# Moving pieces of side work in a two-layer graph network kernel: the last outputs' loads, eight bias additions, two loads of x

## The chip, the cores and the metric

One core of one Trainium2 chip. The metric is the device time of one execution in microseconds (us); the kernel before took a median of 1796.12 us in 3 runs (1794.81 to 1798.48).

## The reference, cut to what matters

```python
# x: (16, 1024, 128), adj: (1024, 1024), all float32
h = relu(layernorm(x))
x = x + (adj @ (h @ weight) + bias)               # layer 0
h = relu(layernorm(x))                            # layer 1
for _ in range(5):
    m  = adj @ h                                  # per batch: (1024,1024) @ (1024,128)
    av = concat([m, m])
    u3 = h @ u3_w.T + u3_b
    z  = sigmoid(av @ w3_w.T + w3_b + u3)
    r  = sigmoid(av @ w4_w.T + w4_b + u3)
    hv = tanh(av @ w5_w.T + w5_b + (r * h) @ u5_w.T + u5_b)
    h  = (1 - z) * h + z * hv
return x + h
```

## The kernel before, in words

The 16 batches go in four quads of four. Two quads are in work at a time and take turns, so that one quad's squares can travel to DRAM and back while the other computes. `step` (L789 on) is one round of one quad; it is written here as (quad, round). The order is (0,0), (1,0), (0,1), (1,1) and so on to (1,4), then (2,0), (3,0) and on to (3,4), which is the last. Within (0,1) and (1,3) an extra aggregation of layer 0 for quads 2 and 3 stands after the gates (`BLOCKS`).

A step has two stages. **The aggregation** (`aggregate`, L436 on) multiplies by adj with two levels of Strassen's scheme: 7 large products, each of 7 small ones, 49 in all (`SMALL`). A small product is 4 matrix multiplications (two 128x256 ones, each in two passes in the trace). Their left sides ("big", "little") are sums that VectorE makes just ahead of use; their right sides are precomputed. Nine of the right sides stay in SBUF ("resident"). The other 40 are streamed from DRAM as 20 pairs of 512 KB through a ring that holds six pairs: `stream()` (L294) issues the next load after every second streamed product. When an aggregation begins, its first six pairs are there, and it issues the loads of the other fourteen itself and, unless it is the last, of the next one's first six. ScalarE takes each result out of PSUM (L519), and VectorE adds it up into mT (L238). Large product 5 of 7 has three such additions of 1024 columns in a row, before which and after which "little" sums of the next products stand. **The gates** (`gates`, L711 on) are 20 multiplications of 512 columns (two passes each) with the weights for each half of the quad, A and then B, with Sigmoid and Tanh on ScalarE and products and sums on VectorE; at their end the new h is transposed in 32x32 squares by VectorE (L581, "sq") and stored to DRAM ("fn").

Side work is put among all this by hand. `put(k, piece)` books a piece, and `place(k)` emits it: `place(1)` to `place(49)` follow the small products of the aggregation, `place("Ar0")`, `"Az3"`, `"Br0"` and the like follow the units of the gates (r for the reset gate, z for the update gate, number of the unit 0 to 3). All that is emitted stays in program order on its engine, and every DMA is issued by SyncE (SP), in order.

The side work that the change touches:

- `put_statistics` (L678 on): layer norm for a coming quad's batches (8 to 15 in its form "a"), the statistics in the gates of one step, the ReLU in the aggregation of the next step. After it, the bias of layer 0 is added to the batch's x (`bias`, L647: one VectorE addition of 1024 columns, "xt<-xt,gb"), at places 26 and 36 of that same aggregation. This happens in (1,0), (0,1), (0,3) and (1,3).
- `LOADS` (L83): loads of later batches' x.
- In the step (3,4), "final": the outputs of quad 2 (`output`, L627). Each has three pieces. load: the last h comes back from DRAM in four gathering DMAs of 128 KB ("ho<-fn"), and x in one of 512 KB ("xt<-x1d"); rest: x is added ("xt<-xt,ho", two additions on VectorE); store. The load of the first stands in the gates of (2,4) ("Bz1"). The flip pool, from which "ho" and "sq" are taken, has three buffers.
- `squares` of the fourth batch of a quad is booked for place 3 of the next aggregation, and the stores of the third and fourth batch's squares for places 4 and 9 (in `turn`, L838).

Of the kernel before, what the change touches and what calls it, by code (L numbers as in the profile page):

```python
# [47 lines left out]
def _small_products():  # L48
# [33 lines left out]
}  # L82
LOADS = {  # L83
    (0, 0): ((8, 25), (9, 34), (10, 43), (11, "Ar0")),
    (0, 2): ((12, 26), (13, 40)),
    (1, 2): ((14, 26), (15, 40)),
}
TRANSPOSED = {(1, 0): 1, (1, 4): 2, (3, 0): 3}
OUTPUTS = {(3, 0): 0, (2, 1): 1, (3, 1): 2, (2, 2): 3, (3, 2): 4, (2, 3): 5, (3, 3): 6, (2, 4): 7}
# [4 lines left out]
def tile_two_gnn_layers(  # L94
# [30 lines left out]
    def dma(out, in_):  # L125
        pin(nc.sync.dma_start(out=out, in_=in_))
# [4 lines left out]
    def x_tile(b):  # L131
        return pre.tile([P, NC, D], F32, tag="xt", name=f"xt_{b}")

    def load_x(b, xt=None, parts=((0, NC),)):
        xt = xt if xt is not None else x_tile(b)
        for cs in parts:
            cs = slice(*cs)
            dma(xt[:, cs], by_slots(x[b])[:, cs])
        return xt
# [97 lines left out]
    def add(o, a, b):  # L237
        pin(nc.vector.tensor_add(o, a, b))  # L238
# [190 lines left out]
    def early_pieces(n):  # L429
        bigs, smalls = left_pieces(n)  # L430
        return bigs[0] + smalls[0] + bigs[1] + bigs[3]

    def period(i):
        return 2 + 7 * i
# [132 lines left out]
    def flip_tile(nm):  # L567
        return flip.tile([P, NSQ, NC, SQ], F32, tag="sq", name=nm)
# [34 lines left out]
    def transposing(b, hT):  # L603

        box = {}

        def load():
            box["sq"] = flip_tile(f"sqt_{b}")
            dma(box["sq"].rearrange("p k j e -> p (k j e)"), parked[b][0])

        def turn():
            for g in range(NH):
                pin(nc.vector.transpose(transposed_half(hT, g), squares_of_half(box["sq"], g)))

        return load, turn
# [4 lines left out]
    def put(k, *pieces):  # L620
        fixed.setdefault(k, []).extend(pieces)
# [25 lines left out]
    def bias(b):  # L647
        both = gb.unsqueeze(1).to_broadcast([P, NC, D])
        add(xts[b], xts[b], both)
# [28 lines left out]
    def put_statistics(kind, first):  # L678

        rest = []  # L680
        for n, b in enumerate((first, first + 1)):
            box = {}

            def begin(b=b, box=box):
                box["n"] = Norm(xts[b], None, f"{kind}{b}")
                box["n"].statistics(range(CH))

            def relu(k, b=b, box=box):
                def run():
                    if k == 0:  # L690
                        box["n"].dst = flip_tile(f"h{kind}_{b}")
                    box["n"].relu(range(2 * k, 2 * k + 2))

                return run

            def done(b=b, box=box):
                (keep if kind == "a" else layer_1_input)(b, box["n"].dst)

            key = "AB"[n]
            put(f"{key}r3", begin)  # L700
            put(f"{key}z1", lambda box=box: box["n"].statistics(range(CH, NC)))
            put(f"{key}z3", lambda box=box: box["n"].scales(EVERY))
            rest.append((10, lambda box=box: box["n"].shift(EVERY)))
            rest += [(11 + 13 * n + 3 * k, relu(k)) for k in range(CH)]
            rest.append((22 + 14 * n, done))
            if kind == "a":
                rest.append((26 + 10 * n, lambda b=b: bias(b)))
        return rest


# [73 lines left out]
    def loads_of_next(source, places):  # L784

        for k, at in enumerate(places):
            put(at, lambda k=k: natural_from(source[k], nat[:, k]))

    def step(i, loads_at=(period(4), period(5), "Ar0", "Ar2"), early_places=GATE_PLACES):  # L789
        st = state[i]  # L790
        quad, n = st["quad"], st["step"]
        nm = f"{quad}_{n}"
        hT = [hT_all[:, i, k] for k in range(Q)]
        last = n == STEPS - 1
        final = last and quad == quads - 1
        other = state[1 - i]
        me = (quad, n)
        for k, piece in relus.pop("next", ()):
            put(k, piece)
        for b, k in LOADS.get(me, ()):  # L800
            put(k, lambda b=b: xts.update({b: load_x(b)}))
        if me in TRANSPOSED:
            q = TRANSPOSED[me]
            for k in range(Q):
                load, turn_it = transposing(q * Q + k, hT_all[:, q % 2, k])
                put(8 + 10 * k, load)
                put(17 + 10 * k, turn_it)
        if me in OUTPUTS:
            for k, piece in zip((16, 34, 38), outputs[OUTPUTS[me]]):
                put(k, piece)  # L810
        block = BLOCKS.get(me)

        source = h0_of(block) if block else other["blocks"]
        if final:
            st["x1"] = []

            def load_x1(k):
                x1 = x_tile(f"1_{quad * Q + k}")
                dma(x1, x1s[quad * Q + k])
                st["x1"].append(x1)  # L820

            for k, places in enumerate(((None, 10, 13), (2, 18, 21), (15, 28, 31), (24, 40, 43))):
                for piece, at in zip(outputs[(quad - 1) * Q + k], places):
                    if at is not None:
                        put(at, piece)
            for k, at in enumerate((17, 34, "Ar0", "Ar3")):
                put(at, lambda k=k: load_x1(k))
        if source is not None:
            loads_of_next(source, loads_at)
        aggregate(nm, place)  # L830
        if me in NORMS:
            relus["next"] = put_statistics(*NORMS[me])
        if source is not None:
            for k, piece in zip(early_places, early_pieces(made[0])):
                put(k, piece)
        stored, ready = {}, {}

        def turn(first):  # L838
            def run(k):
                k += first  # L840
                stored[k] = Later(lambda n: ready[k][n])

                def squares():
                    store, ready[k] = squares_to_dram(hT[k], f"{nm}_{k}")
                    if k >= Q - 2:
                        put({Q - 2: 4, Q - 1: 9}[k], store)
                    else:
                        store()

                if k == Q - 1:  # L850
                    put(3, squares)
                else:
                    squares()

            return run

        if last:
            outputs.update({quad * Q + k: output(quad * Q + k, Later(lambda n, k=k: ready[k][n])) for k in range(Q)})
            if quad == quads - 2:
                put("Bz1", outputs[quad * Q][0])  # L860
        for a, key in enumerate("AB"):
            pair = slice(2 * a, 2 * a + 2)
            if final and a == 1:
                for k, (load, rest) in enumerate(final_outputs(quad, st, stored)):
                    put(f"Br{2 * k}", load)
                    put(f"Bz{2 * k + 1}", rest)
            gates(
                [mT[:, 2 * a + k] for k in range(2)],
                hT[pair],
                f"{nm}{key}",  # L870
                key,
                turn(2 * a),
                finish=finish(quad, hT[pair], st) if final and a == 1 else None,
            )
        if final:
            st["quad"], st["blocks"] = None, None
            return
        st["step"] += 1
        st["blocks"] = [stored[k] for k in range(Q)]
        if last:  # L880
            begin(i, quad + 2)
        if block:
            loads_of_next(other["blocks"], (period(3) + 4, period(4) + 4, period(5) + 2, period(6)))
            pieces = early_pieces(made[0] + 1)
            for k, piece in zip(BLOCK_PLACES, pieces):
                put(k, piece)
            aggregate(f"a{block}", place)
            for k in range(Q):
                for g in range(NH):
                    po(block * Q + k, g)  # L890
                    if 2 * k + g in (1, 2, 6, 7):
                        pieces[{1: 6, 2: 7, 6: 8, 7: 9}[2 * k + g]]()
# [4 lines left out]
    def begin(i, quad):  # L897

        if quad >= quads:
            state[i] = {"quad": None, "blocks": None}  # L900
            return
        state[i] = {"quad": quad, "step": 0, "blocks": parked_of(quad)}
# [13 lines left out]
    def h0_of(quad):  # L916
        return Later(lambda k: h0_blocks[quad * Q + k])
# [151 lines left out]
    for k in range(Q):  # L1069
        b = Q + k  # L1070
# [56 lines left out]
```

## Time and profile before

| | |
|---|---|
| median of 3 runs | 1796.12 us |
| profiled execution | 1800.02 us, of it 1798.2 us span |
| TensorE busy | 1776.1 us (99%) |
| VectorE, ScalarE busy | 1364.2 us (76%), 901.3 us (50%) |
| mean DMA rate | 220 GB/s |
| gates, both halves | 34.34 us |
| aggregation without a wait of TensorE | 42.36 us |

The gates' first multiplications (line L720, "pr") stand in the chain of work that ended last. From one such start to the next is one step's length:

| step | from | to | length | over 76.70 |
|---|---|---|---|---|
| most | 1208.49 | 1285.18 | 76.69 | 0 |
| (1,0) | 176.71 | 257.32 | 80.61 | 3.91 |
| (0,1) | 257.32 | 334.95 | 77.63 | 0.93 |
| (0,2) | 461.17 | 539.98 | 78.81 | 2.11 |
| (1,2) | 539.98 | 616.91 | 76.93 | 0.23 |
| (0,3) | 616.91 | 694.53 | 77.62 | 0.92 |
| (1,3) | 694.53 | 772.16 | 77.63 | 0.93 |
| (1,4) | 898.52 | 976.40 | 77.88 | 1.18 |
| (3,0) | 1053.10 | 1131.79 | 78.69 | 1.99 |
| (3,4) | 1668.70 | 1752.21 | 83.51 | 6.81 |

The names in a row of the trace leave out buffer and batch numbers, so "ring<-rd" is any load of the ring and "pr_4A" any quad's round 4, half A. "x4" is the number of instructions merged in a row. In square brackets stands the idle time of the engine before the row and what ended it.

### The profile page before, as it was taken

Reading aid. Unit: us, or ns where it says so; the run is one execution under the profiler, and the core shown is the slowest. Engines: PE = TensorE matmul, PEld = TensorE weight load, DVE = VectorE, ACT = ScalarE, POOL = GpSimd, SP = SyncE. Lnnn points to the kernel's source line nnn. Section 1 sums busy time; section 2 is a strip of 40 time slices with the busy share of each in tenths; the row PEclk is TensorE's granted clock in tenths of the full one; section 3 lists DMA queues with packets and bytes.
Section 4 is the critical chain, followed back from the end, with each engine's and each line's share of the span. In section 5 each row is a group of like instructions: output and inputs, shape, how many; then the busy total and the mean of one; then the engine's idle time right before and its main releaser. Section 6 shows DMA issues by size and latency. Waiting matters only on the chain.

```text
span 1798.2 us, 21453 instructions
## 1 busy us (share of the span) xinstructions
PE 1776.1 (99%) x6466; PEld 1208.7 (67%) x6466; DVE 1364.2 (76%) x2793; ACT 901.3 (50%) x1969; POOL 57.3 (3%) x41
## 2 busy tenths in 40 slices
PE   9999999999999999999999999999999999999998
PEld 3558576678585766758857667585675857668574
DVE  5758879676878697877687968778686776877776
ACT  5226555544555655554455554545455454454534
POOL 2101000000000000000000000000000000000000
PEclk9999999999999999999999999999999999999999
DMA  6399684678485956649839477494865849577592
GB/s 219 132 340 307 220 294 155 209 221 250 150 276 171 313 170 207 228 134 287 254 125 340 160 238 253 157 324 134 243 214 173 276 140 286 169 217 244 159 333 94
DMA packets 168866, 396.36 MB, mean 220 GB/s; under 512 B 18480, under 2 KB 86960, under 8 KB 168752
## 3 DMA queue, kind: packets, MB, share of 16 engines
q1 hardware_dynamic: 168752, 395.00, 68.0%
q8 instruction: 52, 0.85, 0.2%
q14 instruction: 62, 0.51, 0.1%
HBM read 314.18 MB, written 80.74 MB: 220 GB/s over the span
## 4 chain that ended last, share of the span: by engine, by line
PE 91%; DVE 4%; DMA 3%; issue 1%; ACT 1%; POOL 0%; SPq 0%; DVEq 0%; POOLq 0%; ACTq 0%
PE a L500 25%; PE c L500 12%; PE b L500 6%; PE pq_a L543 4%; PE a_a L500 3%; PE pr_0A L720 2%; PE pr_3B L720 2%; PE pr_2A L720 2%; PE pr_1A L720 2%; PE pr_4A L720 2%; PE pr_3A L720 2%; PE pr_2B L720 2%; PE pr_1B L720 2%; PE pr_0B L720 2%; PE pr_4B L720 2%; PE pv_2A L720 2%
## 5 line engine op out<-in xcount | busy, mean ns | idle before, releaser
L500 PE MATMUL a<-ring,big 128*128 128x256 f32 x1120 | 289.6, 381 | 2.2 <-DMA ring<-rd 1.6
L519 ACT COPY Z<-a 128x256 f32<-128x256 f32 x480 | 177.4, 371 | 210.7 <-PE a L500 208.7
L238 DVE TENSOR_TENSOR Z<-Z,taps 128x512 f32<-128x512 f32 (+1 forms) x264 | 144.3, 553 | 143.4 <-ACT taps L519 143.4
L500 PE MATMUL c<-ring,little 128*128 128x256 f32 x960 | 247.3, 380 | 0.6 <-DMA ring<-rd 0.6
L500 PEld LDWEIGHTS a<-ring,big 128*128 128x128 f32 x1120 | 213.2, 191 | 39.9 <-issue 10.1
L238 DVE TENSOR_TENSOR mT<-mT,Z 128x1024 f32<-128x1024 f32 x154 | 186.7, 1224 | 44.4 <-ACT Z L519 39.8
L500 PEld LDWEIGHTS c<-ring,little 128*128 128x128 f32 x960 | 182.8, 191 | 26.0 <-ACT Z L519 0.9
L519 ACT COPY taps<-c 128x256 f32<-128x256 f32 x280 | 103.7, 370 | 119.5 <-PE c L500 114.6
L500 PE MATMUL a<-ring,little 128*128 128x256 f32 x560 | 146.0, 383 | 9.0 <-DVE little L235 9.0
L500 PE MATMUL a<-resident,little 128*128 128x256 f32 x560 | 144.1, 380 | 0.0
L500 PE MATMUL b<-ring,big 128*128 128x256 f32 x560 | 143.8, 379 | 0.0
L500 PEld LDWEIGHTS a<-ring,little 128*128 128x128 f32 x560 | 105.3, 191 | 27.6 <-ACT taps L519 8.2
L500 PEld LDWEIGHTS a<-resident,little 128*128 128x128 f32 x560 | 107.0, 191 | 14.8
L500 PEld LDWEIGHTS b<-ring,big 128*128 128x128 f32 x560 | 106.3, 190 | 14.9 <-DMA ring<-rd 0.4
L581 DVE STREAM_TRANSPOSE sq<-hT_all 128x512 f32<-128x512 f32 x156 | 101.2, 686 | 4.2 <-DMA fn<-sq 4.2
L398 ACT COPY big<-nat 128x512 f32<-128x512 f32 x132 | 80.6, 614 | 0.1
L519 ACT COPY taps<-b 128x256 f32<-128x256 f32 x140 | 52.1, 372 | 56.8 <-PE b L500 54.6
L235 DVE TENSOR_TENSOR little<-little,big 128x256 f32<-128x256 f32 x154 | 65.4, 425 | 6.7
L235 DVE TENSOR_TENSOR little<-big 128x256 f32<-128x256 f32 x154 | 64.2, 417 | 0.0
L235 DVE TENSOR_TENSOR little<-big,little 128x256 f32<-128x256 f32 x154 | 64.2, 417 | 0.0
L238 DVE TENSOR_TENSOR little<-big 128x256 f32<-128x256 f32 x154 | 63.9, 415 | 0.3 <-ACT big L398 0.2
L519 ACT COPY mT<-a 128x256 f32<-128x256 f32 x80 | 29.8, 373 | 47.5 <-PE a L500 47.5
(250 smaller groups left out, 2911.4 us busy)
## 6 DMA issues: line engine op xcount, KB each, us to landing
ring<-rd SPq DMA_DIRECT2D x440, 512.0 KB, 6.3
fn<-sq SPq DMA_DIRECT2D x78, 512.0 KB, 3.3
nat<-fn SPq DMA_DIRECT2D x256, 128.0 KB, 7.0
x1d<-xt SPq DMA_DIRECT2D x16, 512.0 KB, 5.6
sqt<-ft SPq DMA_DIRECT2D x16, 512.0 KB, 7.2
xt<-x1d SPq DMA_DIRECT2D x16, 512.0 KB, 7.3
xt<-in_x_dram SPq DMA_DIRECT2D x15, 512.0 KB, 5.6
ho<-fn SPq DMA_DIRECT2D x56, 128.0 KB, 6.5
```

What stands on the lines that cost most here:

```text
L235: pin(nc.vector.tensor_sub(o, a, b))
L238: pin(nc.vector.tensor_add(o, a, b))
L398: return [lambda i=i: pin(nc.scalar.copy(made_of(k, i), part(a, b, i))) for i in range(2)]
L500: nc.tensor.matmul(bank, l, right[:, c, :], start=opens and c == 0, stop=c == SB - 1, skip_group_check=True,)
L519: pin(nc.scalar.copy(to, bank))
L543: nc.tensor.matmul(bank, hN[i][:, c, :], raw[c // SB][g][:, c % SB], start=c == 0, stop=c == NC - 1,)
L581: pin(nc.vector.transpose(squares_of_half(sq, g), transposed_half(hT, g)))
L720: nc.tensor.matmul(bank, w_sb[:, w, :], moving, start=start, stop=stop, skip_group_check=True)
```

## The change

It moves pieces and adds none. The eight bias additions go from places 26 and 36 of the aggregation to "Ar0" and "Br0" of the gates of the same step. The loads of x for batches 13 and 15 go from place 40 to "Ar1". In (3,4) the loads of the second, third and fourth output of quad 2 go from places 2, 15 and 24 to 12, 18 and 28, their additions from 18, 28 and 40 to 24, 31 and 42, their stores from 21, 31 and 43 to 27, 34 and 45, and one load of quad 3's x from 34 to 36.

```diff
 LOADS = {
     (0, 0): ((8, 25), (9, 34), (10, 43), (11, "Ar0")),
-    (0, 2): ((12, 26), (13, 40)),
-    (1, 2): ((14, 26), (15, 40)),
+    (0, 2): ((12, 26), (13, "Ar1")),
+    (1, 2): ((14, 26), (15, "Ar1")),
 }
...
             if kind == "a":
-                rest.append((26 + 10 * n, lambda b=b: bias(b)))
+                rest.append((("Ar0", "Br0")[n], lambda b=b: bias(b)))
...
-            for k, places in enumerate(((None, 10, 13), (2, 18, 21), (15, 28, 31), (24, 40, 43))):
+            for k, places in enumerate(((None, 10, 13), (12, 24, 27), (18, 31, 34), (28, 42, 45))):
                 for piece, at in zip(outputs[(quad - 1) * Q + k], places):
                     if at is not None:
                         put(at, piece)
-            for k, at in enumerate((17, 34, "Ar0", "Ar3")):
+            for k, at in enumerate((17, 36, "Ar0", "Ar3")):
                 put(at, lambda k=k: load_x1(k))
```

## The prediction

> **What bounds the kernel now.** I read the page first, then the waits of TensorE, then the step lengths in the chain of work that ended last (the table above), and the timelines around each wait that I found.
>
> ```profile
> PE 1776.1 (99%) x6466; PEld 1208.7 (67%) x6466; DVE 1364.2 (76%) x2793; ACT 901.3 (50%) x1969; POOL 57.3 (3%) x41
> ...
> PE a L500 <- DVE little L235: 9.0, 7, 2.8
> ...
> PE a L500 <- DMA ring<-rd: 1.6, 1, 1.6
> ```
>
> TensorE bounds it, and the change takes no matrix work away. So all that can be won is TensorE's waits and what follows them. The lengths over 76.70 in the table sum to 19.0 us. Seven waits for "little" sums (total us, times, longest) make 9.0 of it directly.
>
> The longest waits cost more than their own length. In (1,0) and in (3,4):
>
> ```profile
> 249.65 0.42 DVE L235 TENSOR_TENSOR little<-little,big 128x256 f32<-128x256 f32 x1
> ...
> 250.22 1.12 PE L500 MATMUL a<-ring,little 128*128 128x256 f32 x4 [1.93 <-DVE little L235]
> ...
> 251.16 1.89 PE L500 MATMUL a<-ring,big 128*128 128x256 f32 x4
> ...
> 255.43 1.03 PE L500 MATMUL c<-ring,little 128*128 128x256 f32 x4
> ```
> ```profile
> 1715.31 1.30 DVE L581 STREAM_TRANSPOSE sq<-hT_all 128x512 f32<-128x512 f32 x2 [4.23 <-DMA fn<-sq]
> ...
> 1719.64 2.07 PE L500 MATMUL a<-ring,little 128*128 128x256 f32 x4 [2.80 <-DVE little L235]
> ...
> 1726.18 1.03 PE L500 MATMUL c<-ring,little 128*128 128x256 f32 x4
> ```
>
> Four passes take 1.03 us as a row (0.865 from start to start). After the 1.93 us wait they run at half speed until about 254.5: from 250.22 to 255.43 are four small products, 5.21 instead of 3.46, so 1.75 lost on top. After the 2.80 us wait the four from 1719.64 to 1726.35 take 6.71, so 3.25 lost on top. The 1.63 us wait for a ring load in (0,2) is followed by full speed. So here a wait of some 1.9 us or more costs another 1.75 to 3.25.
>
> In (3,4) VectorE stood 4.23 us before the fourth batch's square, since its buffer was still being stored ("fn<-sq", issued at 1708.07, landed 7.2 later). The wait at 1719.64 follows.
>
> **What the Trainium skill says.** "TensorE: Matmul & The Clock Gate", Part 1, has the array at half clock after an idle window of about 3.4 us and at full clock again after as much work; the trace agrees on the halving and on 3.5 and 6.5 us of it (twice the losses), but here 1.93 us of idle are enough. "DMA: Bandwidth & Descriptors", Queues, rings and completion order, has each DMA engine take the descriptors of one issuing engine's ring in order: so what is queued ahead decides when a load lands. The loads' landing in the order of issue agrees. The same page, Bandwidth, has 435 GB/s as the ceiling; single microseconds of this trace reach 434. "VectorE: DVE Perf Modes", section The TRN2 errata, gives (N+151)/0.96 ns for a float32 addition: 1224 ns for 1024 columns, measured 1218.
>
> **The bias additions, in the aggregation.** Each is 1.22 us of VectorE. The one at 26 meets no wait: VectorE stands idle 2.0 us soon after (clean steps show 2.02 and 2.35). The one at 36 stands right before the three long additions of large product 5, and the "little" sums that come after them are late for the 44th small product. (0,1), (0,3) and (1,3) wait 0.8, 0.7 and 0.8 us there and nowhere else. Their excess 0.93 + 0.92 + 0.93 = 2.78 goes. (1,0) also has two square transposes (1.29 us) at place 37, which stay. Its twins without a bias, (1,4) and (3,0), wait 1.0 us; (1,4) is 1.18 over. So (1,0) goes from 3.91 to 1.18, and loses the half clock: 2.73. Together 5.51 us. Nothing is late next: in (1,0) and (0,1) the last ring loads land at 247 to 248 and 328, needed at 249.1 to 251.7 and 329.7 or later.
>
> **The bias additions, in the gates.** At Ar0 VectorE has 1.02 us idle before each of three r products and 0.69 before the first update in A: 3.75 against 1.22, hidden. In B, with statistics too:
>
> ```profile
> 287.26 0.69 DVE L759 TENSOR_TENSOR hv_0B<-hv_0B,hT_all 128x512 f32<-128x512 f32 x1 [0.31 <-ACT hv_0B L755]
> ...
> 364.89 0.69 DVE L759 TENSOR_TENSOR hv_1B<-hv_1B,hT_all 128x512 f32<-128x512 f32 x1 [2.60 <-ACT hv_1B L755]
> ```
>
> In (0,1) and (1,3) the 2.60 us hide it. In (1,0) and (0,3) only 0.31 do: VectorE leaves the gates 0.91 later and has no gap before the next aggregation's sums. The first one due is "little" for the 10th product. It ends at 297.82 and is needed at 299.44, its weights some 0.2 before; in (1,3) it ends at 735.03, needed at 736.65. 1.62 - 0.2 - 0.91 leaves 0.5. I take nothing; without that slack it costs up to 0.9 in each of two steps.
>
> **The two loads of x.** The (0,2) wait at 535.43 is for a ring load issued at 526.51, long before the load that moves (540.41). So that wait stays. On SP's queue the move frees the ring loads at 540.85 and puts 512 KB (1.3 us) ahead of the fourth gather for the next product, which isn't needed before Bz1, some 25 us on. Batches 13 and 15 are read in the next steps' gates. Nothing; bounds -0.3 to +0.3.
>
> **The last step.** In the built order the fourth square's buffer no longer comes from the third's store but from the second's, landed long ago. VectorE's 4.23 us and the wait of 2.80 + 3.25 go. VectorE's later places fit: an addition at 24 or 31 precedes idle times of 2.02 and 2.35, and at 42 it delays a sum by 1.28 to about 39.3 us into the stage, where it is needed at 40.6. But what is late next? The queue of loads:
>
> ```profile
> 1712.00:1722.00 10.00, 7.20 (x29) 5.84 (x28) 6.59 (x14) 2.46 (x8) 0.00 (x0) 0.84 0.95 360
> 1722.00:1732.00 10.00, 10.00 (x39) 8.48 (x38) 8.71 (x17) 3.53 (x11) 0.00 (x0) 0.81 1.02 358
> 1732.00:1742.00 10.00, 10.00 (x48) 8.80 (x47) 5.56 (x12) 5.12 (x14) 0.00 (x0) 1.00 1.05 344
> ...
> 1725.16 0.32 SPq L126 DMA_DIRECT2D ring<-rd  x1
> ...
> 1743.34 1.10 PE L500 MATMUL a<-ring,big 128*128 128x256 f32 x4 [0.58 <-ACT taps L519]
> ```
>
> The last two numbers of a window are DMA share and GB/s: for 30 us the DMA engines are full. The stage starts at 1703.03. Its 8th ring load (1725.16) lands 7.9 later, at 1733.06. It serves the 32nd product, which an unhindered TensorE starts 31 x 0.865 = 26.8 after the start, at 1729.85. The late start of before hid those 3.2 us. The 11th landed 8.8 after 1734.4, at 1743.2, which is the 0.58 us wait (put down to ScalarE, long done). The 12th landed at 1744.4, unhindered due at 1739.35.
>
> The new order has the same 15 transfers ahead of the 8th ring load (seven ring loads, two squares, two gathers, three loads of x, one store), and the same 22 ahead of the 12th. Only the 11th gets past two. The second output's load starts 10 us later, but the queue keeps 6 of those filled with ring loads and squares; its idle time early in the stage, about 1 us by my count, replaces the 0.7 it lost while SP waited for VectorE. So I take the landings as they were, within 0.7. Then TensorE waits 2.5 to 3.9 us for the 8th, runs at half clock after it (1.75 to 3.25), and the 12th allows no less than 4.4 to 5.1 in all. Sum 5.0 to 6.8, taken 5.8, instead of 6.8: a gain of 1.0.
>
> From the gates of (3,4) to the end nothing is moved but a store (43 to 45), before a chain of additions and gathers that doesn't use it.
>
> **Sum.** 5.5 + 0 + 0 + 1.0 = 6.5. The profiled execution would go from 1800.0 (span 1798.2 and 1.8 around it) to 1793.5; it lies 3.9 above the median of the runs, which goes from 1796.1 to 1789.6.
>
> **The rivals.** (a) The queue holds nothing up: all of the 6.0 us of VectorE's stall and the 0.6 return. For it: other stages run at a DMA share of 0.94 to 0.98 without a wait. Against it: the landings above. 5.5 + 6.2 = 11.7, so 1784.4. (b) The biases don't fit in B, 0.9 in two steps, and the last step gives nothing: 5.5 - 1.8 = 3.7, so 1792.4. (c) Slower: the starved ring makes a chain in (3,4). Each wait of about 3.1 us brings 3.25 at half clock, and the queue drains no faster meanwhile, since issue waits for freed slots. Two such waits (12.7) against 6.8 are nearly paid by the biases; from three on (19.1) it decides: 12.3 more, less 5.5, so 1802.9. Against it: at half clock the queue catches up, as it did before. (d) That the change doesn't do what it says is excluded for the order: the built program has each piece at its new place.
>
> **Chances.** Forecast 0.61 (1788.0 to 1791.5), (a) 0.2, (b) 0.15, (c) 0.04. The bound of 0.2% is 3.6 us, about what a measurement can tell. Below 1792.5 lie the forecast, (a) and half of (b): faster 0.87; same 0.09, slower 0.04. The range reaches from inside (a) to (b): 1784.0 to 1792.8.
>
> **What would show it.** Right: no wait for "little" in (0,1), (0,3), (1,3), about 1.0 in (1,0); in (3,4) no VectorE wait for "fn<-sq", but a TensorE wait of about 3 us "<-DMA ring<-rd" near 27 us into the stage, with half clock after it, and a stage of 47 to 49 us against 49.2. Wrong: a stage near 42.4 to 44 (a), a "little" wait at the 10th product (b), several ring waits (c).

## The result, and the profile after

The changed kernel takes 1792.99 us, the median of 18 runs (1788.01 to 1798.00), against 1795.92 us for the kernel before in 18 runs (1793.29 to 1802.94). The ratio is 0.9978 (95% interval 0.9969 to 0.9987), so 4.0 us less (2.3 to 5.6). The direction was forecast with 0.87. The size was forecast too large, 6.5 for 4.0. The median, 1793.0 for a forecast of 1789.6, lies 0.2 above the stated range (1784.0 to 1792.8); 4.0 off the 1796.1 that the forecast started from would be 1792.1, inside it but outside the part that the forecast itself had (1788.0 to 1791.5). The 0.22% also stands barely beyond the 0.2% that I had named as the bound of "faster", and its interval reaches below it.

The page of the changed kernel's profile (1793.59 us, span 1791.8) shows TensorE less busy, with the same number of instructions. A small product at half clock counts as busy for longer (a row of four passes below takes 1.92 us instead of 1.03):

```profile
PE 1772.3 (99%) x6466; PEld 1206.8 (67%) x6466; DVE 1363.7 (76%) x2793; ACT 900.2 (50%) x1969; POOL 57.9 (3%) x41
```

TensorE's waits in it (total us, times, longest):

```profile
PE c L500 <- DMA ring<-rd: 5.1, 1, 5.1
PE a L500 <- DVE little L235: 3.6, 4, 1.0
```

The 9.0 us behind "little" have become 3.6, and the longest of them is 1.0 instead of 2.8. In their place stands one ring load of 5.1, where the profile before had a single ring wait of 1.6. The timeline of TensorE and SyncE around it, in the stage of (3,4), which starts at 1696.65:

```profile
1718.69 0.34 SPq L126 DMA_DIRECT2D xt<-x1d  x1
1719.95 5.53 SPq L126 DMA_DIRECT2D ring<-rd  x4
```
```profile
1729.06 2.04 PE L500 MATMUL c<-ring,little 128*128 128x256 f32 x4 [5.12 <-DMA ring<-rd]
1730.89 1.92 PE L500 MATMUL a<-ring,big 128*128 128x256 f32 x4
1732.60 1.62 PE L500 MATMUL a<-resident,little 128*128 128x256 f32 x4
1734.06 1.03 PE L500 MATMUL c<-ring,little 128*128 128x256 f32 x4
```

The 8th ring load is issued at 1719.95 and lands 32.3 us into the stage; the product that it serves, the 32nd, starts at 32.4 instead of 26.8. Three products follow at about half speed. VectorE, on the other hand, has lost its wait of 4.23 us for the square's buffer:

```profile
1704.78 1.30 DVE L581 STREAM_TRANSPOSE sq<-hT_all 128x512 f32<-128x512 f32 x2
```

Step by step, the excess over a clean step (76.70 us, or 126.22 with the extra aggregation) in the two profiles, from the first gate row of one step to that of the next in the timeline; "end" is what follows the last gates' start:

| | (1,0) | (0,1) | (0,2) | (1,2) | (0,3) | (1,3) | (1,4) | (3,0) | (3,4) | end |
|---|---|---|---|---|---|---|---|---|---|---|
| before | 3.92 | 0.92 | 2.12 | 0.23 | 0.92 | 0.93 | 1.18 | 1.99 | 6.80 | 46.16 |
| after | 1.31 | 1.17 | 0.79 | 0.41 | 0 | 0 | 1.19 | 1.23 | 8.05 | 44.73 |

These differences and 0.1 at the start make the 6.4 us between the spans. Five of them I had not forecast: (0,1) doesn't fall and (3,4) rises, while (0,2), (3,0) and the end are 1.3, 0.8 and 1.4 shorter, where I expected nothing of the change. So the forecast for the profiled execution, 1793.5, was met (1793.59) by errors that cancel, and the runs had to tell which of these differences belong to the change.

### The profile page after: what moved, and what is told of

Same layout as the page of the kernel before. It is cut to its first block, busy times and chain, and to the rows that moved or that the text cites. A ratio compares the mean times of both kernels' runs of the same rounds, so it can differ in the third digit from the quotient of the medians.

```text
span 1791.8 us, 21453 instructions
## 1 busy us (share of the span) xinstructions
PE 1772.3 (99%) x6466; PEld 1206.8 (67%) x6466; DVE 1363.7 (76%) x2793; ACT 900.2 (50%) x1969; POOL 57.9 (3%) x41
## 4 chain that ended last, share of the span: by engine, by line
PE 94%; DVE 3%; DMA 2%; ACT 0%; issue 0%; SPq 0%; DVEq 0%; ACTq 0%
PE a L500 26%; PE c L500 13%; PE b L500 6%; PE pq_a L543 6%; PE a_a L500 3%; PE pr_1B L720 2%; PE pr_3B L720 2%; PE pr_2B L720 2%; PE pr_4A L720 2%; PE pr_2A L720 2%; PE pr_1A L720 2%; PE pr_3A L720 2%; PE pr_0A L720 2%; PE pr_0B L720 2%; PE pr_4B L720 2%; PE po L655 2%
```

## The experiments

My theory after reading the profile: the bias additions free the aggregations as forecast; (0,1) waits because VectorE enters the gates of (1,0) late, behind a load; in (3,4) the queue of loads decides. The main rivals: half B has no room for the addition in any case; the lateness of the ring load has another cause than what is queued ahead of it; the loads of x do something.

### One part at a time

The bias additions alone, as an edit of the kernel before:

```diff
-                rest.append((26 + 10 * n, lambda b=b: bias(b)))
+                rest.append((("Ar0", "Br0")[n], lambda b=b: bias(b)))
```

> Only the eight bias additions move to the gates. Theory Q (the biases are the whole gain; the last step's loads give nothing, since the queue of loads holds TensorE there): the steps (1,0), (0,1), (0,3), (1,3) lose 2.6, gain 0.2 and lose 0.9 and 0.9 us of length as in the changed kernel, together 4.2 us, with a wait of some 0.6 us for a left sum at the 10th product of (0,1); the last step stays at 83.5 +- 1 us; time 4 to 5 us below the kernel before. Rival L (the last step's new order is the gain and additions among the gates cost as much as they save): within 1 us of the kernel before.

The places of the last step alone:

```diff
-            ... ((None, 10, 13), (2, 18, 21), (15, 28, 31), (24, 40, 43))):
+            ... ((None, 10, 13), (12, 24, 27), (18, 31, 34), (28, 42, 45))):
...
-            for k, at in enumerate((17, 34, "Ar0", "Ar3")):
+            for k, at in enumerate((17, 36, "Ar0", "Ar3")):
```

> Only the last step's pieces move. Theory Q: VectorE no longer waits for the square's buffer, but TensorE waits 3 to 5 us for the 8th ring load of the stage, 32 us after its start, and runs at half clock after it: the last step's length is 83 to 85 us instead of 83.5, time within 1.5 us of the kernel before. Rival L: the stage comes down to 43 to 45 us (a length of 77.5 to 79), time 5 to 6 us below.

The loads of x alone:

```diff
-    (0, 2): ((12, 26), (13, 40)),
-    (1, 2): ((14, 26), (15, 40)),
+    (0, 2): ((12, 26), (13, "Ar1")),
+    (1, 2): ((14, 26), (15, "Ar1")),
```

> Only the loads of x for batches 13 and 15 move. Theory Q: no step changes by more than the waits for ring loads in (0,2) and (1,2) scatter from one execution to the next (0.2 to 2.1 us in the two profiles), time within 1 us of the kernel before. Rival X (they free SP's queue, which is why (0,2) was 1.3 us shorter in the changed kernel): (0,2) at 77.5 instead of 78.8, time 1 to 1.5 us below.

Measured against the kernel before, with each ratio turned into us of its 1796:

| part | median us (runs) | ratio, 95% | us |
|---|---|---|---|
| bias additions | 1792.87 (12) | 0.9980 (0.9971 to 0.9989) | -3.6 (-5.2 to -2.0) |
| last step's places | 1794.73 (13) | 0.9992 (0.9984 to 1.0000) | -1.4 (-2.9 to 0) |
| loads of x | 1796.56 (13) | 1.0002 (0.9994 to 1.0011) | +0.4 (-1.1 to +2.0) |
| all three | 1792.99 (18) | 0.9978 (0.9969 to 0.9987) | -4.0 (-5.6 to -2.3) |

The parts sum to -4.6, which agrees with the whole. Only the bias additions are clear of noise, and they make most of it; the last step's places may make about a third (their interval reaches 0), and the loads of x nothing that these runs can tell. In the profile of the bias additions alone, (0,3) and (1,3) have no excess and (1,0) has 1.32, but (0,1) keeps 0.41.

In the profile of the last step's places alone the same ring wait appears, two microseconds shorter and with full speed after it, so that (3,4) is only 3.32 over. This execution (1792.35) was the fastest of the 13, so the draw was a lucky one. Its rows:

```profile
1730.16 1.10 PE L500 MATMUL c<-ring,little 128*128 128x256 f32 x4 [3.08 <-DMA ring<-rd]
1731.10 1.03 PE L500 MATMUL a<-ring,big 128*128 128x256 f32 x4
1731.96 1.03 PE L500 MATMUL a<-resident,little 128*128 128x256 f32 x4
```

### Two outputs' loads behind the last ring load

If the queue of loads decides in (3,4), then taking two outputs' loads out of the way of the ring loads must give far more than any spacing. The changed kernel with the loads of the third and fourth output of quad 2 moved to places 34 and 40, behind the stage's last ring load, their additions and stores moved to the gates, and the loads of quad 3's x moved behind the ring loads too:

```diff
-            ... ((None, 10, 13), (12, 24, 27), (18, 31, 34), (28, 42, 45))):
+            ... ((None, 10, 13), (12, 24, 27), (34, "Ar1", "Ar2"), (40, "Az0", "Az1"))):
...
-            for k, at in enumerate((17, 36, "Ar0", "Ar3")):
+            for k, at in enumerate((36, 44, "Ar3", "Az2")):
```

> The changed kernel, with the third and fourth output of quad 2 loaded behind the last ring load (places 34 and 40) and added in the last gates, and with the loads of quad 3's x behind them. Theory Q: only 12 transfers instead of 15 stand ahead of the 8th ring load, one of them a gather, so it lands at about 26 us into the stage, where it is needed; no ring wait over 1.5 us, the stage of the last step at 42.4 to 44 us instead of 50.4, the time 6 to 8 us below the changed kernel. Rival L (something else holds the stage, or the moved pieces come back in the gates and the end): the stage stays over 47 us, or the stretch from the last gates to the end grows from 44.6 to 46 us by as much as the stage wins.

It takes 1785.42 us (6 runs), ratio 0.9939 (0.9926 to 0.9952): 11.0 us less than the kernel before, some 7 less than the changed one. (3,4) is 0.95 over. The ring wait of 5.1 is gone; what is left in that stage, at 24.2 us into it:

```profile
1721.42 1.10 PE L500 MATMUL c<-ring,little 128*128 128x256 f32 x4 [0.72 <-DMA ring<-rd]
```

The loads at 34 and 40 are still issued within the stage. So the queue ahead of the ring loads was the limit, and the 7 us lay in the outputs' and x loads that stood there. The additions moved as well, but the wait that went is one for a ring load.

### One ring load ahead of one output

A finer test of the same: only the third output's load goes behind the 8th ring load, from place 18 to 19.

```diff
-            ... ((None, 10, 13), (12, 24, 27), (18, 31, 34), (28, 42, 45))):
+            ... ((None, 10, 13), (12, 24, 27), (19, 31, 34), (28, 42, 45))):
```

> The changed kernel with the load of the third output (four gathers and 512 KB of x) at place 19 instead of 18, so that the 8th ring load of (3,4) goes ahead of it on SP's queue. Theory (the queue ahead decides when the ring load lands): 1 MB less lies ahead, 2.1 us for the gathers and 1.3 for x by the rates of the stage, so it lands about 28.7 us into the stage instead of 32.1, TensorE waits some 2 us instead of 5.1, and (3,4) is 4.4 to 6.8 over instead of 8.05: 1 to 3.5 us less, as the 12th load still holds it up. Rival (the lateness is that of a ring slot freed late or of the DMA engines' share, not of what is queued ahead): it lands within 0.7 of 32.1, (3,4) stays near 8.

The time is 1790.29 us (5 runs), ratio 0.9967 (0.9954 to 0.9981); the interval overlaps that of the changed kernel, so the gain isn't shown. The profile is of the slowest of the five (1797.28; the others took 1789.52 to 1792.38), so it isn't typical of them. Its stage starts at 1699.49:

```profile
1729.12 1.53 PE L500 MATMUL c<-ring,little 128*128 128x256 f32 x4 [2.70 <-DMA ring<-rd]
...
1743.12 1.93 PE L500 MATMUL b<-ring,big 128*128 128x256 f32 x4 [2.37 <-DMA ring<-rd]
```

The 8th ring load is issued 18.6 us into the stage instead of 23.3, and the 32nd product starts at 29.6 instead of 32.4. That looks like the expected move, but it isn't shown: five executions with the third load at 18 have this start at 30.0 to 32.4 (a table further below), so 29.6 is only 0.4 below the earliest of them. A later ring load is then missing, 43.6 us into the stage, and each of the two waits is followed by half speed: (3,4) is 9.09 over in this execution, not 4.4 to 6.8. I had taken the later loads to cap the stage, and had not counted a second half-speed stretch. VectorE also stood 6.55 us for the x of this output at place 31; TensorE was itself waiting for the ring during part of that.

### Why (0,1) waits

In the changed kernel TensorE waits in (0,1) for the "little" sum of the 10th product:

```profile
297.32 1.13 PE L500 MATMUL a<-ring,little 128*128 128x256 f32 x4 [0.57 <-DVE little L235]
```

VectorE makes that sum late, because it has entered the gates of (1,0) late. TensorE's first gate row, the issue of the load and VectorE's timeline, first before and then after:

```profile
257.16 1.02 PE L720 MATMUL pr_0A<-mT,w_sb 128*128 128x512 f32 x2
250.28 0.43 SPq L126 DMA_DIRECT2D sqt<-ft  x1
255.44 1.30 DVE L613 STREAM_TRANSPOSE hT_all<-sqt 128x512 f32<-128x512 f32 x2 [0.72 <-DMA sqt<-ft]
```
```profile
254.48 1.02 PE L720 MATMUL pr_0A<-mT,w_sb 128*128 128x512 f32 x2
252.07 0.43 SPq L126 DMA_DIRECT2D sqt<-ft  x1
258.05 1.30 DVE L613 STREAM_TRANSPOSE hT_all<-sqt 128x512 f32<-128x512 f32 x2 [5.19 <-DMA sqt<-ft]
...
280.28 1.21 DVE L238 TENSOR_TENSOR xt<-xt,gb 128x1024 f32<-128x1024 f32 x1
...
286.71 0.68 DVE L759 TENSOR_TENSOR hv_0B<-hv_0B,hT_all 128x512 f32<-128x512 f32 x1
```

The fourth square of the quad's h is loaded at place 38 and transposed at 47, the end of the aggregation. In the changed kernel's profile the transposes start 3.57 us after TensorE has begun the gates (254.48), where before they started 1.7 us ahead of them. About half of these 5.3 us is TensorE's: without its old wait it begins the gates 2.7 us earlier. The other half is the load, which lands 2.6 us later in this execution. Over the four executions with the additions at the old places and the six with them in the gates and this load at 38, the mean entries differ by 3.6 us: counted from the span's start, TensorE is 2.4 earlier and the load 1.2 later. In the changed kernel's profile VectorE then has no idle time left to the end of the gates, not even the 0.31 ahead of hv_0B, and it begins the next aggregation late.

Two runs were to separate this from a lack of room in half B. One puts both additions in half A of the changed kernel:

```diff
-                rest.append((("Ar0", "Br0")[n], lambda b=b: bias(b)))
+                rest.append((("Ar0", "Ar1")[n], lambda b=b: bias(b)))
```

> The changed kernel with its second bias addition at Ar1 instead of Br0. In its profile (0,1) waits 0.57 us for the little sum of the 10th product and is 1.17 over 76.70. Theory 1 (VectorE enters (1,0)'s gates too late, after 5.19 us of waiting for the fourth square load, and has no idle time left in either half): the addition costs its 1.22 us in A as it did in B, so (0,1) keeps 0.4 to 1.2 over, (0,3) stays at 0. Theory 2 (it was half B that had no room, as my rival b had it): A has some 2.5 us of idle time beside the additions, so (0,1) loses its excess, 1.2 us less in all. Time within 0.1% of the changed kernel by theory 1, 1 us less by theory 2.

It takes 1792.11 us (6 runs), ratio 0.9980 (0.9968 to 0.9993). In its profile (0,1) has no excess, as theory 2 wanted; but VectorE entered the gates 1.6 us earlier in that execution, relative to TensorE, so this run can't tell the two apart, as the table below shows. The other issues the load before the gathers of "nat" instead of after them, and leaves the addition in half B:

```diff
-                put(8 + 10 * k, load)
+                put((8, 18, 28, 35)[k], load)
```

> The changed kernel with one more move: the fourth square load of (1,0), (1,4) and (3,0) from place 38 to 35, ahead of the gathers of nat on SP's queue. Theory (the little wait in (0,1) comes from VectorE's 5.19 us wait for this load at the end of (1,0)): the load is issued near 246 us instead of 252 and lands before 253, VectorE's wait shrinks from 5.2 to 1 or less, VectorE enters the gates 2.5 us or more earlier, and (0,1) falls from 1.17 to 0.3 or less. Rival (the bias at Br0 alone makes it, whatever the entry): (0,1) keeps 0.9 to 1.2. Time: 0.5 to 1.2 us less than the changed kernel, at the edge of what can be told from the runs.

It takes 1791.33 us (12 runs), ratio 0.9975 (0.9965 to 0.9985), no gain over the changed kernel that these runs can tell. The mechanism shows in the profile. The timeline of SyncE and VectorE in this kernel:

```profile
241.52 0.32 SPq L126 DMA_DIRECT2D sqt<-ft  x1
243.97 0.32 SPq L126 DMA_DIRECT2D ring<-rd  x1
```
```profile
253.15 1.30 DVE L613 STREAM_TRANSPOSE hT_all<-sqt 128x512 f32<-128x512 f32 x2
258.11 1.22 DVE L238 TENSOR_TENSOR xt<-xt,gb 128x1024 f32<-128x1024 f32 x1
260.93 0.69 DVE L733 TENSOR_TENSOR r_0A<-r_0A,hT_all 128x512 f32<-128x512 f32 x1 [1.00 <-ACT r_0A L732]
```

In the changed kernel the load was issued at 252.07, here at 241.52. VectorE meets no wait, has idle time again at the r products, and (0,1) has no excess with the addition still at Br0. All executions with the additions among the gates, by the start of these transposes relative to TensorE's first gate row of (1,0):

| kernel | entry, us | (0,1) over |
|---|---|---|
| load at 35 | -1.71 | 0 |
| load at 35, outputs in the gates (the last kernel below) | -1.36 | 0 |
| changed kernel, again | +0.98 | 0 |
| both additions in A | +2.00 | 0 |
| outputs in the gates | +2.42 | 0 |
| bias alone | +2.78 | 0.41 |
| changed kernel | +3.57 | 1.17 |
| third load behind ring | +4.63 | 2.25 |

Up to about +2.4 us nothing is lost, and beyond that each microsecond of lateness costs about one. So half B has room for the addition when VectorE enters the gates in time. Lateness alone costs little: (1,4) and (3,0) load their fourth square in the same way and have no bias addition, and in the ten executions with that load at 38 their gates are entered 2.0 to 5.0 us late, yet the step after is at most 0.39 over, and that at the latest entry.

### Both profiles a second time

> The kernel before, profiled a second time, unchanged. Theory (part of what set its first profile 3.9 us above the median was chance: half speed at the end, 46.2 us from the last gates' start instead of 44.6, and a ring wait in (0,2), 2.12 over): (1,0) again 3.9 over, (0,1), (0,3), (1,3) again 0.92 each, (3,4) 6.5 to 8.5; but (0,2) under 0.3 or the end near 44.6, or both, and a span of 1792 to 1797. Rival (these belong to the kernel before): (0,2) again near 2.1 and the end near 46, span 1797 to 1799.

> The changed kernel, profiled a second time, unchanged. Theory: (1,0) 1.3 over, (0,3) and (1,3) at 0, (0,1) between 0 and 2.3 as VectorE enters (1,0)'s gates earlier or later than 3 us after TensorE, and the 8th ring load of (3,4) lands 30 to 31 us into the stage, as in the two other kernels with these places, not at 32.2, so that (3,4) is 3.3 to 6 over; the span 1786 to 1792. Rival (the landing at 32.2 belongs to the kernel as it stands): within 0.7 of 32.2, (3,4) 7.5 to 8.5 over.

The kernel before again: 1798.12 us, span 1796.3. (0,1), (0,3) and (1,3) are 0.93 over each, (3,4) 7.13. The end takes 44.47 us instead of 46.16, as the theory had it, but (0,2) is 2.02 over again and (1,2) 2.24, which it had not. So the short end is chance (it took 46.03 and 46.21 with the bias additions alone and with the outputs in the gates); the ring waits of (0,2) and (1,2) recur here, though in the two kernels with the loads of x at their old places (bias alone, last step alone) the pair summed to 0.51 and 0, in the run that moved only those loads to 0.22, and in the changed kernel to 1.20 and, a second time, 1.65. What makes them I can't say.

The finding that I had not expected stands in (1,0). The first row is the same to the hundredth as in the first profile of before, and the wait as long (1.94 for 1.93), yet full speed follows it:

```profile
250.22 1.10 PE L500 MATMUL a<-ring,little 128*128 128x256 f32 x4 [1.94 <-DVE little L235]
251.16 1.03 PE L500 MATMUL a<-ring,big 128*128 128x256 f32 x4
252.02 1.03 PE L500 MATMUL c<-ring,little 128*128 128x256 f32 x4
```

(1,0) is 2.25 over in this execution, and 3.92 in the other.

The changed kernel again: 1792.21 us, span 1790.4, (1,0) 1.32, (0,1), (0,3) and (1,3) 0, (3,4) 5.79 with its 32nd product at 30.8 us into the stage. So the landing at 32.3 isn't a fixed property of the kernel. (3,0) is 3.75 over here, where 1.23 stood in the first profile; a ring wait of 1.64 is the larger part of the difference.

### A kernel faster than both

What remained were waits of 1.0 us for "little" in (1,0), (1,4) and (3,0), at the product that the bias at 36 used to hold up as well: the third pair of square transposes stands at place 37 behind the three long additions. The kernel with the outputs in the gates, with these transposes at 43 and the early fourth load:

```diff
-                put(8 + 10 * k, load)
-                put(17 + 10 * k, turn_it)
+                put((8, 18, 28, 35)[k], load)
+                put((17, 27, 43, 47)[k], turn_it)
```

> The changed kernel with the outputs of quad 2 in (3,4)'s gates as in the earlier run (1785.4 us), and with two more moves in (1,0), (1,4), (3,0): the third pair of square transposes from place 37, right behind the three long additions, to 43, and the fourth square load from 38 to 35. Theory (the waits of 1.0 us for little at the 44th product come from the transposes at 37, and the late gates of (1,0) from the fourth load): the three excesses of 1.3, 1.2 and 1.5 go, 3 to 4 us less than in that earlier run, so about 1781.8. Rival: the transposes delay the additions of the last large product and so the gates instead, same time as that earlier run.

It takes 1781.38 us (6 runs, 1780.11 to 1787.37), ratio 0.9923 (0.9909 to 0.9937): 13.8 us less than the kernel before (11.3 to 16.3). That is 2.9 less than without these two moves by the ratios and 4.0 by the medians. The two intervals overlap, though five of the six runs lie below the lowest of the six without the moves (1783.62). TensorE's waits of 0.5 us or more in it:

```profile
PE pf L953 <- DVE hT_all L761: 2.4, 2, 2.0
PE pq_a L543 <- DMA big<-in_adjT_dram: 1.6, 2, 0.8
PE unread L146 <- DVE zeros L143: 1.4, 1, 1.4
PE po L655 <- ACT mT L554: 0.7, 1, 0.7
PE a L500 <- ACT Z L519: 0.5, 1, 0.5
```

No wait for "little" or for the ring is left. In VectorE's timeline of (1,0) the "little" sums follow the long additions at once, and the transposes fit behind them:

```profile
243.15 3.62 DVE L238 TENSOR_TENSOR mT<-mT,Z 128x1024 f32<-128x1024 f32 x3 [0.31 <-ACT Z L519]
246.69 0.42 DVE L238 TENSOR_TENSOR little<-big 128x256 f32<-128x256 f32 x1
...
248.75 1.30 DVE L613 STREAM_TRANSPOSE hT_all<-sqt 128x512 f32<-128x512 f32 x2
```

(1,0) is 0.14 over, (1,4) 0, (3,0) 0.85, (3,4) 0.15. Without the two moves the first three were 1.31, 1.18 and 1.46.

## Why the prediction was right in direction and too large in size

**The bias additions, in the aggregation: right, with a term too large.** (0,3) and (1,3) lost their 0.92 and 0.93 in every execution with the additions moved, and (1,0) went to 1.31, forecast 1.18. But I took 3.91 as what (1,0) costs before. Its half clock came in three of four executions with the old places (3.92, 3.94, 3.94 and 2.25, mean 3.5), so 0.4 of the 2.73 was a throw of the dice that I had read as a rule.

**The bias additions, in the gates: this step failed.** "I take nothing; without that slack it costs up to 0.9 in each of two steps" had the right place, the 10th product, and the wrong quantity. I had computed how much later VectorE leaves the gates from the 1.22 us added in B and the 0.31 idle there, and kept its entry into the gates as it was. The entry moved: with the old wait gone from (1,0), the fourth square's load is what comes last, and VectorE entered 1.0 to 4.6 us after TensorE, where the profile that I read had it 1.7 ahead. "Nothing is late next: in (1,0) ... the last ring loads land at 247 to 248" looked at TensorE's loads and left out VectorE's. In the five executions that have the additions at Ar0 and Br0 and that load where it was, (0,1) is 0.41, 1.17, 0, 2.25 and 0 over, mean 0.77. Of the 0.93 forecast to go there, 0.16 goes.

With both corrections the 5.5 becomes 4.2 (3.5 - 1.31, 0.93 - 0.77, and 1.85), which the timed 3.6 (2.0 to 5.2) allows.

**The loads of x: right.** +0.4 us (-1.1 to +2.0) for a forecast of nothing.

**The last step: right, and the first profile hid it.** The forecast was a TensorE wait of 2.5 to 3.9 us for the 8th ring load at its old landing, about 30.0 us into the stage, half clock after it, and 5.0 to 6.8 over, taken 5.8. Five executions with these places:

| kernel | 32nd product starts, us into the stage | TensorE's wait | (3,4) over |
|---|---|---|---|
| changed kernel | 32.4 | 5.1 | 8.05 |
| changed kernel, again | 30.8 | 3.9 | 5.79 |
| last step alone | 30.0 | 3.1 | 3.32 |
| both additions in A | 30.9 | 4.0 | 5.87 |
| load at 35 | 30.2 | 3.3 | 5.24 |

Their mean excess is 5.7. With the old places the four executions have 6.80, 7.81, 8.44 and 7.13, mean 7.5. That is a gain of 1.9 by profiles and 1.4 (0 to 2.9) by time, for a forecast of 1.0. Three of the working's figures were off, without changing what was forecast. It mixed two clocks of the profile: the times of the chain lie some 0.16 us behind those of the timeline, so the half clock after the wait of 2.80 cost 3.1 (from 1719.64 to 1726.18), not 3.25, and the landing was 30.2 us into the stage. Its terms, 2.5 to 3.9 and 1.75 to 3.25, add to 4.3 to 7.2, not to 5.0 to 6.8. And its tolerance for the landing (0.7) was too narrow: 29.9 to 32.3 was measured.

**The transfer to the median: this failed too.** I let the profiled execution's 3.9 us above the median stand, as if the kernel carried it. The end at half speed is some 1.7 of it and didn't recur when the same kernel was profiled again; the changed kernel's profile lies 0.6 above its own median. So a matching profile (1793.5 forecast, 1793.59 measured) and a median 3.4 above the forecast go together.

**The rivals.** (a), a queue that holds nothing up, is excluded by the ring wait in all five executions; it came near only where two outputs' loads stood behind the last ring load. Its own terms, 6.0 and 0.6, make 6.6 rather than the 6.2 that it used. (b), biases that don't fit in B, gave the nearest number, 1792.4, but not for its reasons: (0,3) never waited, (0,1) waited only behind a late load, and the last step seems to have given something (1.4, 0 to 2.9). (c), a chain of ring waits, didn't happen in the changed kernel; with the third load behind the ring it began in the one execution profiled, two waits with half speed after each, and stopped short of the three that (c) needed.

**Left open.** Corrected as above, the sum is 4.2 + 1.4 to 1.9, so 5.6 to 6.1, and the timed whole is 4.0 (2.3 to 5.6). The difference may be scatter, since single executions of one kernel lie 10 us apart; no run here decides it. Nor is it shown what makes a ring load land 29.9 us into the stage in one execution and 32.3 in another, nor why the fourth square's load lands at 254.8 in one execution of the changed kernel and at 258.0 in another.

## What to carry to other kernels

Before pricing an added instruction by the idle time beside it, ask what the engine's entry into that stretch hung on: where a wait is removed, the next one may be a load that another engine waits for, and an idle time seen in the old trace isn't there in the new. Where the DMA queue is full through a stage, spacing the loads within the queue gave little here (1.4 us, 0 to 2.9); putting the side loads behind the last load that a product waits for took the wait away (7 us more). And an excess in one profile, above all one behind a wait of about two microseconds, can be a draw: profile the same kernel twice before it goes into a sum.

## What the hardware showed that I had not expected

**Half clock after a short wait is not a matter of the wait's length alone.** At the end of the kernel TensorE waits for "hT_all" in all twelve executions profiled, for 1.78 to 2.14 us. Three are followed by half speed (waits of 2.07, 1.90 and 2.08) and nine are not, the longest among them. The same piece of the kernel before and of the changed one:

```profile
1786.89 1.80 PE L953 MATMUL pf<-ident,hT_all 128*128 128x128 f32 x8 [2.07 <-DVE hT_all L761]
1788.49 1.06 PE L720 MATMUL pv_4B<-mT,w_sb 128*128 128x256 f32 x2
```
```profile
1781.99 1.13 PE L953 MATMUL pf<-ident,hT_all 128*128 128x128 f32 x8 [2.14 <-DVE hT_all L761]
1782.95 0.60 PE L720 MATMUL pv_4B<-mT,w_sb 128*128 128x256 f32 x2
```

The two multiplications of the second row take 1.06 us in one and 0.60 in the other. The waits of 2.37 to 5.12 us in (3,4) were followed by half speed in ten cases of eleven; the eleventh is the 3.08 above. Ten waits of 1.36 to 1.69 us in the aggregations of these executions were not followed by it. The Trainium skill ("TensorE: Matmul & The Clock Gate", Part 1) calls the window over which activity is judged free-running, and so the effect different from run to run; these runs agree with that, while its figure of at least one idle window of about 3.4 us doesn't fit halvings after 1.9 us. So my sentence "a wait of some 1.9 us or more costs another 1.75 to 3.25" should have carried a chance.

**A DMA share of one says little about the bytes.** The windows of the kernel with the outputs in the gates, in (3,4) (the last three numbers are TensorE's clock, DMA share and GB/s):

```profile
1707.00:1717.00 10.00, 10.00 (x48) 8.81 (x47) 9.76 (x21) 4.39 (x12) 0.00 (x0) 1.00 1.02 298
1717.00:1727.00 10.00, 9.28 (x44) 7.88 (x43) 6.37 (x14) 4.86 (x13) 0.00 (x0) 1.00 1.03 413
1727.00:1737.00 10.00, 10.00 (x48) 8.67 (x47) 7.32 (x12) 4.34 (x12) 0.00 (x0) 1.00 1.04 295
```

At the same full share 298, 413 and 295 GB/s were moved. What SyncE had issued shortly before the middle window were six ring loads in a row; ahead of the others stand gathers of 128 KB, squares and stores as well. That these make the difference is argued, not shown.
